# First-layer value weights loaded from GpSimd's queue, and an exponential of one element before the first conversions, in a two-layer attention kernel

## The chip, the cores and the metric

The kernel runs on one core of a Trainium2 chip. The metric is the time of one execution on the device, in microseconds (us). A core has five engines that run side by side: TensorE (PE in the profile; its weight loads are a row of their own, PEld), VectorE (DVE), ScalarE (ACT), GpSimd (POOL) and SyncE (SP). Transfers between the chip's memory and the core's are issued by SP, ACT and POOL, each from a queue of its own, and are carried by 16 DMA engines that all queues share.

## The reference, cut to what matters

Two attention layers over 4 images of 4096 tokens with 256 channels; all numbers are fp32.

```python
# layer 0
q, k, v = x @ Wq + bq, x @ Wk + bk, x @ Wv + bv       # 256 -> 32, 32, 256
attn = softmax(q @ k.T)                               # 4096 x 4096 for each image
x = gamma * (attn @ v) + x
# layer 1
f, g, v = x @ Wf + bf, x @ Wg + bg, x @ Wh + bh       # 256 -> 32, 32, 128
beta = softmax(g @ f.T)
x = x + (beta @ v) @ Wo + bo
```

The weights matter here: Wq and Wk of layer 0 hold 32 KB each, Wv of layer 0 holds 256 KB, Wh of layer 1 holds 128 KB.

## The kernel before, in words

The work of an image and layer is cut into steps: a block of queries (256 in layer 0, 512 in layer 1) against a group of keys. A step computes scores on PE (line 638), exponentials on ACT (a reduced-precision "high" part at line 648 and the whole at 655), differences on DVE (676, 681), and sums weighted by the values on PE (706, 730). From step 8 on the order of all instructions is the order in which the program writes them (`MANUAL_FROM = 8`, line 1138 and around); ahead of that a scheduler orders them, engine by engine, and it also chooses the semaphores that DMAs raise. The queues of SP and ACT share eight such semaphores, and the queue of POOL has eight more; each is used in turn, and an issue whose semaphore still belongs to an earlier DMA waits until that one has landed.

The change lies in the lead, the part before the first scores. There the kernel

- loads the first 8 tiles of tokens from SP (`load_first`, line 311, 128 KB each); tiles 0 and 1 form half-block 0, tiles 2 and 3 half-block 1, and so on;
- makes an identity matrix on POOL (`make_identity`, masks.py:197 and 199);
- loads the weights in the loop of lines 340 to 355: for layer 0 from ACT's queue, for layer 1 from POOL's. In each turn the weights of queries and keys go into one tile `wqk_whole` (line 345), the biases into `bqk` (346), ACT rounds the tile to a "high" part (349), DVE forms the rest (350), and the weights of values are loaded (354). Lines 356 to 358 load three small tensors of layer 1 from POOL;
- for each half-block transposes the tokens on PE (417, result `psx`), copies them to `xT` on ACT (418), rounds them to `xh` on ACT (435), forms `xl` on DVE (438), and projects them: queries and keys on PE (456, `psqk`, from `xh` and `xl` with `wqk`), values on PE (507, `psv`, from `xT` with `wv`);
- takes the projections out: queries and keys by ACT (472), DVE (476), ACT (479) and DVE (483), after which eight small DMAs from POOL spread them into `k` and `q` (line 560); values by ACT (537) and DVE (550, 551).

So ACT's first instructions, before the change, are its issues of Wq, bq, Wk, bk and Wv, then the load of its function table, then the conversion at line 349. In PE's order the first projection of values (507) stands behind the transposes of half-blocks 0 and 1 and ahead of the first projection of queries and keys (456), with which it is interleaved. In ACT's order the value take-out of half-block 0 (537) stands ahead of the second rounding of its queries and keys (479).

The change also names `seen_v`, a small tile that line 333 sets to zero and in which line 517 later notes sizes of values, and `down`, one number per partition that line 332 sets to -2^-13.

Of the kernel before, what the change touches and what calls it, by code (L numbers as in the profile page):

```python
# [50 lines left out]
F32 = mybir.dt.float32  # L51
F32R = mybir.dt.float32r
I32 = mybir.dt.int32
AF = mybir.ActivationFunctionType
# [3 lines left out]
P = 128  # L58
# [192 lines left out]
def fast_path(ctx: ExitStack, tc: tile.TileContext, x, w0, w1, wo, bo, gamma, out, off):  # L251

    nc = tc.nc
    B, N, C = x.shape
    NCC = C // P
    NB = N // QB
    D = w0[0].shape[1]
    CV = (w0[4].shape[1], w1[4].shape[1])
# [14 lines left out]
    const = ctx.enter_context(tc.tile_pool(name="const", bufs=1))  # L273
# [56 lines left out]
    seen_v = const.tile([P, 2, NH], F32, name="seen_v")  # L330
    down = const.tile([P, 1], F32, name="down")
# [4 lines left out]
    wqk, bqk, wv = [], [], []  # L336
    bv1 = const.tile([P, 1], F32, name="bv1")
    gamma_sb = const.tile([P, 1], F32, name="gamma")
    wo_sb = const.tile([P, C], F32, name="wo")
    for l, (q_w, q_b, k_w, k_b, v_w, v_b) in enumerate((w0, w1)):  # L340
        queue = (nc.scalar, nc.gpsimd)[l]
        w_sb = work.tile([P, NCC, 2 * D], F32, tag="small", bufs=4, name=f"wqk_whole{l}")
        b_sb = const.tile([P, 1], F32, name=f"bqk{l}")
        for g, w_dram, b_dram in ((0, q_w, q_b), (D, k_w, k_b)):
            queue.dma_start(w_sb[:, :, g : g + D], w_dram.rearrange("(c p) d -> p c d", p=P))
            queue.dma_start(b_sb[2 * D + g : 3 * D + g, :], b_dram.rearrange("(d o) -> d o", o=1))
        w_parts = const.tile([P, NCC, 4 * D], F32R, name=f"wqk{l}")
        high, low = w_parts[:, :, : 2 * D], w_parts[:, :, 2 * D :]
        nc.scalar.copy(high, w_sb)
        nc.vector.tensor_sub(low, w_sb, high.bitcast(F32))  # L350
        wqk.append(w_parts)
        bqk.append(b_sb)
        v_sb = const.tile([P, NCC, CV[l]], F32, name=f"wv{l}")
        queue.dma_start(v_sb, v_w.rearrange("(c p) d -> p c d", p=P))
        wv.append(v_sb)
    nc.gpsimd.dma_start(bv1, w1[5].rearrange("(c o) -> c o", o=1))
    nc.gpsimd.dma_start(wo_sb, wo)
# [675 lines left out]
    for n, s in enumerate(steps):  # L1033
        now[0] = n
        b, l, j = s.b, s.l, s.j
# [105 lines left out]
def tile_two_attention_layers(tc: tile.TileContext, *args):  # L1141
    nc = tc.nc
    with tc.tile_pool(name="flag", bufs=1) as pool:
        off = pool.tile([1, 1], I32, name="off")
        fast_path(tc, *args, off)
        flag = nc.values_load(off[0:1, 0:1], min_val=0, max_val=4 * P, skip_runtime_bounds_check_because="a count")
        with tc.If(flag < 1, preferred_fallthrough_block=False, label="in_range") as usual:
            pass
        with usual.Else():
            general_path(tc, *args)  # L1150
# [40 lines left out]
```

## Time and profile before

| what | value |
|---|---|
| median of 3 runs | 3091.56 us (3089.11 to 3091.99) |
| the profiled execution's own time | 3090.12 us |
| its span in the trace | 3088.3 us |
| granted TensorE clock, mean | 0.998 |
| PE busy | 3062.8 us, 99% of the span |
| DVE busy | 2765.4 us, 90% |
| ACT busy | 2196.2 us, 71% |
| POOL busy | 772.2 us, 25% |
| ACT_TABLE_LOAD in the whole run | 1, of 1.28 us |

Times in the trace count from the start of the span. The views used are: the page's busy times; the timeline, which gives start, length, engine, line, operation and tiles of each group, and in brackets the engine's idle time before it with what ended it; the table of DMA issues, with each transfer's size and its time from issue to landing; busy time by stretches; and the chain of work that ended last. Rows whose engine ends in q (ACTq, SPq) are issues of transfers. "x4" means that a row merges four instructions.

### The profile page before, as it was taken

The numbers are of one execution on the slowest core, as the hardware profiler recorded it, in microseconds if no ns is written. First come the engines' busy times: TensorE is split into PE (matmuls) and PEld (weight loads), VectorE is DVE, ScalarE is ACT, GpSimd is POOL, SyncE is SP. The second block draws the span as 40 slices with busy tenths as digits, with TensorE's granted clock in tenths as the row PEclk, the third lists the DMA queues.
The fourth block names the chain that finished last, engine by engine and source line by source line (L and its number), as shares of the span: only waits on it lengthen the run. The fifth ranks groups of instructions, "written<-read, shape, count | busy, mean of one in ns | idle before, by whom it ended". The sixth has DMA issues, their size and how long they took to land.

```text
span 3088.3 us, 55083 instructions
## 1 busy us (share of the span) xinstructions
PE 3062.8 (99%) x19866; PEld 2664.2 (86%) x19866; DVE 2765.4 (90%) x3366; ACT 2196.2 (71%) x2900; POOL 772.2 (25%) x1136
## 2 busy tenths in 40 slices
PE   8999999999999999999999999999999999999998
PEld 7999998666799999866689999976668999997665
DVE  7889989999898999999989998999998888889997
ACT  6777777777677777777767677777776666667775
POOL 5111113222421111422241111132234111123332
PEclk9999999999999999999999999999999999999999
DMA  5344445666644444656664444466666333335666
GB/s 134 77 90 88 90 88 117 140 134 137 130 89 90 88 91 87 130 132 137 133 126 92 87 91 88 90 132 130 139 131 118 65 68 73 60 76 118 126 135 142
DMA packets 460902, 331.09 MB, mean 107 GB/s; under 512 B 266610, under 2 KB 404212, under 8 KB 460628
## 3 DMA queue, kind: packets, MB, share of 16 engines
q0 software_dynamic: 109248, 185.47, 33.5%
q1 hardware_dynamic: 350180, 141.47, 18.5%
q8 instruction: 160, 2.62, 0.4%
q14 instruction: 114, 0.93, 0.1%
q10 hardware_dynamic: 1200, 0.59, 0.1%
HBM read 136.58 MB, written 103.61 MB: 78 GB/s over the span
## 4 chain that ended last, share of the span: by engine, by line
PE 90%; DVE 5%; DMA 2%; issue 1%; ACT 1%; POOL 0%; ACTq 0%; DVEq 0%; POOLq 0%
PE acc_pair L706 23%; PE acc L706 23%; PE acc L730 21%; PE st L638 14%; PE psv L507 4%; PE psqk L456 2%; PE pso L838 2%; DMA p_sum_moved<-p 2%; DVE p_sum L695 1%; DVE low L676 1%; DVE d L681 1%; ACT p L655 0%; DVE v0l L681 0%; DVE v0h L676 0%; DVE v0d L676 0%
## 5 line engine op out<-in xcount | busy, mean ns | idle before, releaser
L648 ACT ACTIVATE high<-st,down 128x1024 fp32r<-128x1024 f32 x651 | 727.4, 1117 | 656.4 <-PE st L638 555.2
L655 ACT ACTIVATE p<-st 128x1024 f32<-128x1024 f32 x1024 | 1022.4, 1020 | 30.6 <-DMA p_sum_moved<-p 21.5
L676 DVE TENSOR_TENSOR low<-p,high 128x1024 fp32r<-128x1024 f32 x559 | 683.1, 1222 | 114.6 <-ACT p L655 111.1
L681 DVE SCALAR_TENSOR_TENSOR d<-low,high 128x1024 fp32r<-128x1024 f32 x543 | 662.7, 1220 | 14.6
L638 PE MATMUL st<-q,k 128*128 128x256 f32 (+1 forms) x3072 | 660.3, 323 | 2.2 <-ACT p L655 2.1
L638 PEld LDWEIGHTS st<-q,k 128*128 128x128 f32 x3072 | 469.0, 188 | 60.1 <-issue 13.6
L730 PE MATMUL acc<-p,v 128*128 128x512 f32 (+1 forms) x1028 | 481.4, 590 | 0.2
L706 PE MATMUL acc<-v0d,d 128*128 128x258 f32 x2048 | 336.6, 286 | 0.6 <-DVE d L681 0.6
L706 PE MATMUL acc<-v0h,high 128*128 128x258 f32 x2048 | 329.9, 283 | 0.3 <-ACT o L787 0.3
L706 PE MATMUL acc_pair<-v0h,high 128*128 128x258 f32 x2048 | 330.1, 283 | 0.0
L706 PE MATMUL acc_pair<-v0d,d 128*128 128x258 f32 x2048 | 329.9, 283 | 0.0
L706 PE MATMUL acc_pair<-v0l,low 128*128 128x256 f32 (+1 forms) x2048 | 325.4, 281 | 0.0
L706 PE MATMUL acc<-v0l,low 128*128 128x256 f32 (+1 forms) x2048 | 324.8, 280 | 0.0
L730 PEld LDWEIGHTS acc<-p,v 128*128 128x128 f32 x1028 | 193.2, 189 | 142.6 <-issue 122.8
L771 POOL DMA_DIRECT2D out<-x x128 | 114.4, 894 | 803.2 <-DVE x L765 787.8
L695 DVE TENSOR_TENSOR p_sum<-p_sum,p 128x1024 f32<-128x1024 f32 x253 | 308.4, 1219 | 0.3
L669 POOL DMA_DIRECT2D p_sum_moved<-p x160 | 141.3, 883 | 580.4 <-DMA p_sum_moved<-p 198.4
L706 PEld LDWEIGHTS acc<-v0d,d 128*128 128x128 f32 x2048 | 282.2, 190 | 3.0 <-DVE d L681 1.6
L706 PEld LDWEIGHTS acc<-v0h,high 128*128 128x128 f32 x2048 | 282.3, 190 | 2.1 <-ACT o L787 1.6
L706 PEld LDWEIGHTS acc_pair<-v0h,high 128*128 128x128 f32 x2048 | 281.4, 189 | 0.1
L706 PEld LDWEIGHTS acc_pair<-v0d,d 128*128 128x128 f32 x2048 | 280.7, 189 | 0.1
L706 PEld LDWEIGHTS acc_pair<-v0l,low 128*128 128x128 f32 x2048 | 277.3, 188 | 0.0
(179 smaller groups left out, 4284.1 us busy)
## 6 DMA issues: line engine op xcount, KB each, us to landing
p_sum_moved<-p POOLq DMA_DIRECT2D x193, 512.0 KB, 4.9
x_res<-in_x SPq DMA_DIRECT2D x128, 128.0 KB, 3.2
qk_dram<-qk_parts SPq DMA_DIRECT2D x128, 128.0 KB, 2.0
x_res<-bias POOLq DMA_DIRECT2D x128, 128.0 KB, 4.1
out<-bias SPq DMA_DIRECT2D x128, 128.0 KB, 4.3
out<-x POOLq DMA_DIRECT2D x128, 128.0 KB, 3.1
q<-qk_dram POOLq DMA_DIRECT2D x252, 64.0 KB, 3.8
out<-y POOLq DMA_DIRECT2D x124, 128.0 KB, 4.2
```

The costliest lines, as they stand in the source:

```text
L456: nc.tensor.matmul(t["ps"], wqk[l][:, c, :], x_parts[key][n][:, c, :], start=(c == n == 0), stop=(c == NCC - 1 and n == 1),)
L507: nc.tensor.matmul(ps[:, n, :], xT[key][:, c, n * P : (n + 1) * P], wv[l][:, c, :], start=(c == 0), stop=(c == NCC - 1),)
L638: nc.tensor.matmul(st[:, g, :], k_t[b, l, kt // NT][:, kt % NT * P : (kt % NT + 1) * P], q_t[b, l, j * n // QB][:, q0 : q0 + n], start=Tru ...
L648: nc.scalar.activation(self.high, s_flat, AF.Exp, bias=down)
L655: nc.scalar.activation(self.p, s_flat, AF.Exp)
L669: nc.gpsimd.dma_start(moved_sums[b, j, order % both], self.p, accum_op=ALU.add)
L676: nc.vector.tensor_sub(self.low, self.p, self.high.bitcast(F32))
L681: nc.vector.scalar_tensor_tensor(self.d, self.low.bitcast(F32), -UP, self.high.bitcast(F32), ALU.mult, ALU.add)
L695: nc.vector.tensor_add(p_sum, other, self.p)
L706: nc.tensor.matmul(acc[2 * s + which][:, :width], p[:, g, s * P : (s + 1) * P], v0[self.i][v][:, g, :width], start=self.first and what != ...
L730: nc.tensor.matmul(acc[which].rearrange("p (a n) -> p a n", n=QB0)[:, cols, :], v_part[:, g, :], p[:, g * NS : (g + 1) * NS, :][:, cols, : ...
L771: nc.gpsimd.dma_start(out_rows(b, j, s), x_new, accum_op=ALU.add)
```

## The change

The weights of layer 0's values move ahead of the loop and to POOL's queue. In the loop the two weights of queries and keys are issued first and the two biases after them, for both layers. Between them, for layer 0, ACT computes one exponential per partition from `down` into the first column of `seen_v`, which line 517 overwrites later. Layer 1's weights of values stay where they were.

```diff
+    v0_sb = const.tile([P, NCC, CV[0]], F32, name="wv0")
+    nc.gpsimd.dma_start(v0_sb, w0[4].rearrange("(c p) d -> p c d", p=P))
     for l, (q_w, q_b, k_w, k_b, v_w, v_b) in enumerate((w0, w1)):
         queue = (nc.scalar, nc.gpsimd)[l]
         w_sb = work.tile([P, NCC, 2 * D], F32, tag="small", bufs=4, name=f"wqk_whole{l}")
         b_sb = const.tile([P, 1], F32, name=f"bqk{l}")
-        for g, w_dram, b_dram in ((0, q_w, q_b), (D, k_w, k_b)):
+        for g, w_dram in ((0, q_w), (D, k_w)):
             queue.dma_start(w_sb[:, :, g : g + D], w_dram.rearrange("(c p) d -> p c d", p=P))
+        if l == 0:
+            nc.scalar.activation(seen_v[:, 0, :1], down, AF.Exp)
+        for g, b_dram in ((0, q_b), (D, k_b)):
             queue.dma_start(b_sb[2 * D + g : 3 * D + g, :], b_dram.rearrange("(d o) -> d o", o=1))
...
-        v_sb = const.tile([P, NCC, CV[l]], F32, name=f"wv{l}")
-        queue.dma_start(v_sb, v_w.rearrange("(c p) d -> p c d", p=P))
+        v_sb = v0_sb if l == 0 else const.tile([P, NCC, CV[l]], F32, name=f"wv{l}")
+        if l == 1:
+            queue.dma_start(v_sb, v_w.rearrange("(c p) d -> p c d", p=P))
         wv.append(v_sb)
```

In the scheduled program of the changed kernel ACT's queue begins with Wq, Wk, the table load, the exponential, bq, bk and then the conversion of line 349. POOL's order is: fill of the identity, Wv, the select that finishes the identity, Wg, Wf, bg, bf, Wh, then as before. On PE ten of the first 80 matrix instructions change places, and on DVE and SP a few of the first instructions do (on SP the store of the identity goes ahead of a bias load, and some token tiles ahead of stores); behind that each engine's order is the same in both kernels, and so are the waits, up to the numbering of the semaphores.

## The prediction

> **What bounds the kernel now.** I read the page's busy times first.
>
> ```profile
> PE 3062.8 (99%) x19866; PEld 2664.2 (86%) x19866; DVE 2765.4 (90%) x3366; ACT 2196.2 (71%) x2900; POOL 772.2 (25%) x1136
> ```
>
> PE is idle for 3088.3 - 3062.8 = 25.5 us in all, and the change touches nothing behind the first microseconds: from about the 80th matmul on the scheduled orders are the same. So I ask only how much earlier the lead can hand over to a body that PE fills. Next the timeline of PE (its column: start, length):
>
> ```profile
> 3.32 1.30 PE L417 MATMUL psx<-ident,x_nat 128*128 128x128 f32 x4 [3.32 <-DMA x_nat<-in_x]
> 5.05 1.34 PE L417 MATMUL psx<-ident,x_nat 128*128 128x128 f32 x4 [0.42 <-DMA x_nat<-in_x]
> 8.29 1.19 PE L507 MATMUL psv<-wv,xT 128*128 128x256 f32 x2 [1.90 <-ACT xh L435]
> 8.92 0.78 PE L456 MATMUL psqk<-xh,wqk 128*128 128x256 f32 x1
> 9.49 1.05 PE L507 MATMUL psv<-wv,xT 128*128 128x256 f32 x2
> 9.99 0.78 PE L456 MATMUL psqk<-xl,wqk 128*128 128x256 f32 x1
> 10.56 0.41 PE L456 MATMUL psqk<-xh,wqk 128*128 128x256 f32 x1
> ...
> 13.64 0.28 PE L456 MATMUL psqk<-xl,wqk 128*128 128x256 f32 x1
> ```
>
> PE ends the second transposes at 5.05 + 1.34 = 6.39 and then stands for 1.90 us before the first value projection. The bracket blames the rounding to xh, but psv reads wv and xT, not xh. So I looked at the transfers: issue on ACT, and time to landing.
>
> ```profile
> wv<-in_L_conv_Wv ACTq DMA_DIRECT2D x1, 256.0 KB, 4.8
> wo<-in_L_conv_Wo POOLq DMA_DIRECT2D x1, 128.0 KB, 4.2
> wqk_whole<-in_L_conv_Wg POOLq DMA_DIRECT2D x1, 32.0 KB, 3.4
> wqk_whole<-in_L_conv_Wk ACTq DMA_DIRECT2D x1, 32.0 KB, 3.7
> ```
>
> ```profile
> 0.84 0.46 ACTq L345 DMA_DIRECT2D wqk_whole<-in_L_conv_Wq  x1
> 1.33 0.48 ACTq L346 DMA_DIRECT2D bqk<-in_L_conv_bq  x1
> 1.43 0.88 POOL L345 DMA_DIRECT2D wqk_whole<-in_L_conv_Wg  x1 [0.40 <-issue]
> 1.84 0.45 ACTq L345 DMA_DIRECT2D wqk_whole<-in_L_conv_Wk  x1
> 3.39 0.38 ACTq L354 DMA_DIRECT2D wv<-in_L_conv_Wv  x1
> 3.80 1.28 ACT L349 ACT_TABLE_LOAD   x1 [3.80 <-DMA wqk_whole<-in_L_conv_Wq]
> 5.60 0.30 ACT L349 CAST wqk<-wqk_whole 128x128 fp32r<-128x128 f32 x1 [0.51 <-DMA wqk_whole<-in_L_conv_Wk]
> 5.80 0.58 ACT L418 COPY xT<-psx 128x512 f32<-128x512 f32 x1
> ```
>
> Wv lands at 3.39 + 4.8 = 8.19, and PE starts 0.1 us later. xT was there at 5.80 + 0.58 = 6.38. So the wait is for Wv. It went out late because its issue stood behind four others and, I infer, waited for Wq's landing (0.84 + 2.5 = 3.3), whose semaphore it takes over.
>
> Last, the chain of work that ended last, in order of time, for what hangs on this start:
>
> ```profile
> 11.19 1.72 PE psv L507 x4
> 12.93 0.60 ACT v0h L537
> 13.55 0.41 ACT qk_parts L479
> ```
>
> psv of half-block 0 ends at 12.9; ACT waits for it, and only behind it rounds queries and keys, which start POOL's eight spreading DMAs at 14.24. These go out until 18.15 and take 2.6 us to land (20.75); at 20.87 ACT uses their buffer again. All of that hangs on when psv starts.
>
> **The change part by part.**
>
> *Wv on POOL's queue.* It takes the place of Wg, first on POOL: issue at 1.43 instead of 3.39, 1.96 us earlier. With its own 4.8 us it lands at 6.23. Bounds: not before 4.83, where the 32 KB of Wg landed from this slot; not after 9.9, where Wo, the last large load of this queue, landed (5.69 + 4.2). I take 6.23, since the 4.8 are those of the same bytes. PE then is held by what is next: xT (below, 5.95) and its own transposes (6.39). So psv starts at 6.39 + 0.1 = 6.5: 8.29 - 6.5 = **1.8 us earlier**.
>
> *The cost in the shared DMA engines.* From 4 to 8 us they are 0.97 to 0.99 busy, and now 256 KB come in ahead of token tiles 2 and 3, which held the second transposes for 0.42 us. All of Wv ahead of them would be 256 KB at 294 GB/s (the stretch 6 to 8) = 0.9 us; none, 0. I take 0.3, a third, because the queues of SP and ACT carry bytes beside it. Net **1.5 us**.
>
> Here the Trainium skill speaks against the change: DMA: Bandwidth & Descriptors, "Issuing engines are not separate DMA queues", says that all issuers share the same 16 engines and that spreading issues over several saves the sequencer's time alone. By that the move would be worth 1.96 us of issue at most, and nothing in bandwidth. The busy share of 0.99 agrees.
>
> *Wk ahead of bq.* Wk takes bq's slot: 1.84 to 1.33, 0.5 us earlier, landing at 1.33 + 3.74 (its row in the chain) = 5.07. The conversion goes from 5.60 to about 5.1, xT from 6.38 to 5.1 + 0.30 + 0.58 = 5.95, xh to 6.6, xl (0.69) to 7.3. The second matmul of queries, third on PE from 6.5, needs xl at 7.6, so it is ready. This gain is needed so that xT does not take Wv's place, but adds nothing to the 1.8.
>
> *The exponential.* It pulls the table load from 3.80 to about 1.85, ending at 3.1. The load ended at 5.08 before, 0.5 us ahead of Wk's landing, so it was hidden: worth nothing. Its own length has no row; between 0.15 us (the one-element conversion at line 896) and 0.37 us (an ACTIVATE of 128x256) it is done by 3.5. It fits in a wait of ACT that lasts to 5.07. Without that cover it would cost 1.6 us. There is still one table load, with the same table, so no function needs another.
>
> *The biases, and POOL's other loads.* bq and bk go out at about 3.5 and 4.0 instead of 1.33 and 2.31; at 3.5 us to landing they are there by 7.5, and DVE's line 476 needs them at 11.62 - 1.5 = 10.1. Cover 2.6 us. Wg and Wf now queue behind Wv on POOL; Wf goes from 3.17 to about 3.4 and, at 4.1 us to landing plus up to 0.9 behind Wv, lands between 7.5 and 8.4. ACT's second conversion, at 7.41 before, waits for it, and xh of half-block 1 behind it; but ACT's next (472) waits for PE until about 9.7, and PE reads that xh at 13.40 - 1.5. Hidden. The identity stays where it was, behind one POOL issue. bv, Wo and gamma come about 0.7 us later; DVE reads them behind work that is not due.
>
> *SP.* Token tile 8 was issued at 8.21, just behind Wv's landing at 8.19: it appears to take over Wv's semaphore. It now follows a bias, landed by about 7.5. Tile 6 now follows Wk instead; both feed transposes past 10 us. Nothing is lost.
>
> **Sum.** 1.8 - 0.3 = 1.5 us, carried by the chain above into a body that is PE-bound and unchanged. Against the profiled execution: 3090.12 - 1.5 = **3088.6 us**. That execution is 1.4 under the median of the runs shown and 1.0 over their lowest.
>
> **The rivals.**
>
> *The clock comes up sooner.* The same 256-column matmul takes 0.78 us at 8.92 and 9.99, 0.41 at 10.56 and 0.28 at 13.64, though the granted clock of these stretches reads 1.00. So PE is slow from 8.29 to 10.5, 2.2 us. If it is a pause of PE that makes it slow, a start at 6.5 with hardly a pause halves that: 1.1 more, 2.6 in all, **3087.5**. If the rise falls at the same instant, 10.5, PE does 4.0 us of slow work instead of 2.2: (4.0 - 2.2) / 2 = 0.9 gained, 3089.2. The Trainium skill (TensorE: Matmul & The Clock Gate, Part 1) has a gate that opens after about 3.4 us of sustained activity, in a window that runs freely. By it either end is possible; no run here shows the window.
>
> *POOL's queue is served late.* From 3 to 6 us its packets took 7.6% of the DMA engines, against 51% for SP's. If Wv keeps to such a share, it lands with the last loads, at 9.9, psv starts at 10.0, 1.7 us late: **3091.8, slower**. It decides from a landing after 8.19. Against it: POOL had little but 128-byte pieces out then, and had up to 74% from 7.5 to 8 once Wh and Wo were moving.
>
> *Hidden anyway.* The chain passes through ACT, DVE, POOL's issues and token tiles before PE fills up (PE is idle 0.75 of 4 us from 20, 0.31 from 24). If one of those has its own time, the gain is eaten: **3090.1**. For it: ACT is busy 3.88 of 4 us from 20. Against: all of them start from line 479, which moves along.
>
> **How the numbers follow.** Forecast 0.45, clock sooner 0.15, hidden 0.15, late 0.14, and 0.11 for something no row shows (0.07 faster, 0.04 slower by over 0.2%). 0.2% is 6.2 us, about what a measurement of this kernel can tell from no change; all four named cases lie within it. Range: low end 3090.1 - 2.9 (1.8 + 1.1) less the 1.0 by which runs lie under the profiled one, 3086; high end 3091.8 plus the 1.9 by which the highest run lies over it, 3093.7.
>
> **What would show it.** Right: Wv issued on POOL near 1.4 and landed before 7; psv's first matmul near 6.5 with hardly idle time before it; line 479 near 12.0; the first scores (20.42) near 19; the same PE busy time in the body. Wrong: psv later than 8.3 with Wv landing last; second transposes past 5.9; a wait at line 472 or 476 for a bias; more than one table load; or a body that differs.

## The result and the profile after

The changed kernel takes **3086.85 us** (median of 22 runs, 3084.45 to 3089.01), the kernel before 3090.99 us (22 runs beside them, 3088.08 to 3093.45). The ratio is 0.9987, 95% interval 0.9981 to 0.9992: 4.1 us less, under 0.2%. That is inside the range of the prediction, near its low end of 3086, and 2.7 times the 1.5 us that it forecast. The profiled execution took 3085.12 us, its span is 3083.3 us; before, they were 3090.12 and 3088.3.

Lines of the changed kernel are six higher than before from the transposes on (417 is 423, 456 is 462, 507 is 513, 655 is 661, 667 is 673). First the busy times on the page of the kernel after.

```profile
PE 3061.6 (99%) x19866; PEld 2665.0 (86%) x19866; DVE 2763.9 (90%) x3366; ACT 2198.8 (71%) x2901; POOL 775.3 (25%) x1137
```

PE's idle time fell from 25.5 to 21.7 us. ACT has one instruction more, and so has POOL: 1137 for 1136, since Wv is now its to issue. The second number decides most of what follows.

The lead, in the timeline of PE and in that of ACT with its issues (kernel after; start, length, engine, line, operation, idle time before):

```profile
6.00 1.15 PE L423 MATMUL psx<-ident,x_nat 128*128 128x128 f32 x4 [1.38 <-DMA x_nat<-in_x]
6.94 1.06 PE L513 MATMUL psv<-wv,xT 128*128 128x256 f32 x2
7.44 0.77 PE L462 MATMUL psqk<-xh,wqk 128*128 128x256 f32 x1
...
9.08 0.41 PE L462 MATMUL psqk<-xh,wqk 128*128 128x256 f32 x1
```

```profile
1.32 0.49 ACTq L347 DMA_DIRECT2D wqk_whole<-in_L_conv_Wk  x1
1.84 1.28 ACT L349 ACT_TABLE_LOAD   x1 [1.84 <-issue]
...
3.13 0.20 ACT L349 ACTIVATE seen_v<-down 128x1 f32<-128x1 f32 x1
3.95 0.30 ACT L354 CAST wqk<-wqk_whole 128x128 fp32r<-128x128 f32 x1 [0.61 <-DMA wqk_whole<-in_L_conv_Wk]
4.65 0.59 ACT L424 COPY xT<-psx 128x512 f32<-128x512 f32 x1 [0.40 <-PE psx L423]
...
12.07 0.40 ACT L485 CAST qk_parts<-qk_parts 64x256 fp32r<-64x256 f32 x1
```

And its table of DMA issues (KB, us to landing):

```profile
wv<-in_L_conv_Wv POOLq DMA_DIRECT2D x1, 256.0 KB, 4.3
...
wqk_whole<-in_L_conv_Wk ACTq DMA_DIRECT2D x1, 32.0 KB, 2.5
```

Wv goes out at 1.43 and lands at 5.73. psv now follows the second transposes without idle time, at 6.94 instead of 8.29. What is late next is token tiles 2 and 3: PE stands for 1.38 us before the transposes that need them, which begin at 6.00 instead of 5.05.

To see how far this carries I compared, exponential by exponential (the 1024 of line 655, then 661), how much earlier each begins than in the kernel before. The first begins 1.22 us earlier, the 8th 0.87, the 65th 0.85, the 705th and still the 759th 1.09; in between it wanders (1.95 at the 256th). At the 760th alone it jumps to 3.99, at the 769th it is 4.50, and it stays near that to the end (4.53 at the last). The last stretch but one shows it in busy times too. Rows of kernel before, then after, over the same work (the columns: the stretch, its length, busy us of PE, PEld, DVE, ACT and POOL, clock, DMA share, GB/s):

```profile
84.00:2300.00 2216.00, 2211.22 (x14476) 1934.01 (x14475) 2020.46 (x2424) 1602.06 (x2131) 527.27 (x759) 1.00 0.54 110
2300.00:2350.00 50.00, 47.13 (x178) 31.36 (x177) 40.02 (x42) 33.39 (x47) 28.80 (x49) 1.00 0.71 145
```

```profile
83.10:2298.90 2215.80, 2211.70 (x14476) 1934.38 (x14476) 2019.52 (x2424) 1603.81 (x2131) 528.98 (x759) 1.00 0.54 110
2298.90:2345.50 46.60, 46.17 (x178) 31.73 (x177) 39.93 (x42) 33.64 (x47) 28.86 (x49) 1.00 0.76 155
```

178 matmuls each, in 50.0 us and in 46.6: PE's idle time there was 2.87 us and is 0.43; the other 0.96 of the 3.4 us lie in rows that the view counts as busy. So most of the gain lies 2300 us behind the change, among instructions that it does not touch. What happens there is on POOL. Kernel before, then after:

```profile
2306.95 4.61 POOL L560 DMA_DIRECT2D k<-qk_dram  x8
2316.00 0.56 POOL L667 DMA_DIRECT2D p_sum_moved<-p  x1 [4.45 <-issue]
2316.55 1.96 POOL L560 DMA_DIRECT2D k<-qk_dram  x4
2321.23 0.92 POOL L669 DMA_DIRECT2D p_sum_moved<-p  x1 [2.72 <-DMA p_sum_moved<-p]
...
2327.95 0.92 POOL L669 DMA_DIRECT2D p_sum_moved<-p  x1 [3.82 <-DMA p_sum_moved<-p]
```

```profile
2305.89 4.12 POOL L566 DMA_DIRECT2D k<-qk_dram  x7
2310.68 0.50 POOL L566 DMA_DIRECT2D k<-qk_dram  x1 [0.68 <-DVE v0l L687]
2313.45 0.56 POOL L673 DMA_DIRECT2D p_sum_moved<-p  x1 [2.27 <-ACT p L661]
...
2317.15 0.92 POOL L675 DMA_DIRECT2D p_sum_moved<-p  x1 [1.19 <-ACT p L661]
...
2323.08 0.92 POOL L675 DMA_DIRECT2D p_sum_moved<-p  x1 [3.01 <-DMA p_sum_moved<-p]
```

Eight k loads go out evenly before; after, the eighth is late (the bracket names `v0l` of DVE, which this load does not read). In exchange the first `p_sum_moved`, which copies an exponential away, is not. The pair of exponentials ahead of it on ACT, and the copy in the table of DMA issues, before and after:

```profile
2312.64 1.93 ACT L655 ACTIVATE p<-st 128x1024 f32<-128x1024 f32 x2
p_sum_moved<-p POOLq DMA_DIRECT2D x1, 512.0 KB, 4.6
```

```profile
2311.55 1.93 ACT L661 ACTIVATE p<-st 128x1024 f32<-128x1024 f32 x2
p_sum_moved<-p POOLq DMA_DIRECT2D x1, 512.0 KB, 3.1
```

Before, the second of the pair ended at 2314.57 (2312.64 + 1.93), and the copy went out 1.43 us later, for the blame "issue", that is for nothing the profile names. After, it ends at 2313.48 (2311.55 + 1.93) and the copy goes out with its end. The copy also lands sooner, 3.10 us from its issue for 4.62. Together this is 1.43 + 1.52 = 2.95 us, and the 760th exponential, the next one that waits for this copy, gains 2.90. Why the late copy takes longer to land is open. The next ones add into the same place (lines 667 and 669), so each waits for the one before to land, and ACT waits with the next exponential until the copy of an earlier one has landed. ACT and PE, kernel before, in that order:

```profile
2320.73 1.03 ACT L655 ACTIVATE p<-st 128x1024 f32<-128x1024 f32 x1 [2.79 <-DMA p_sum_moved<-p]
...
2327.45 1.02 ACT L655 ACTIVATE p<-st 128x1024 f32<-128x1024 f32 x1 [2.71 <-DMA p_sum_moved<-p]
```

```profile
2328.52 0.72 PE L638 MATMUL st<-q,k 128*128 128x512 f32 x2 [1.20 <-ACT p L655]
```

After, ACT waits 0.23 us at the second place, and this wait of PE is gone. Over the whole body the views of waits (us, times, longest), first before, then after, have:

```profile
ACT p L655 <- DMA p_sum_moved<-p: 21.5, 12, 3.0
...
PE st L638 <- ACT p L655: 2.1, 2, 1.2
```

```profile
ACT p L661 <- DMA p_sum_moved<-p: 12.2, 10, 2.8
```

**Why one issue is late.** When POOL's DMAs are numbered in the trace, one is late at regular places. At numbers 371, 613, 734 and 1097 of the kernel before a spreading load of k or q (line 560) stands directly behind another, and goes out 1.60, 1.55, 1.52 and 1.72 us behind it; the places are 121 apart or multiples of it. Elsewhere this kernel has 451 such pairs, and in 420 the distance is under 0.8 us. Late pairs elsewhere move with the program: those at 171, 443, 715 and 987 (1.84 us each) are at 172, 444, 716 and 988 in the kernel after (1.76 to 1.83). In the twelve traces of this study (before, after and ten experiments) 55 such pairs fall on the series 129 + 121 n, and all 55 are 1.43 us apart or more (the most 3.31). It is not the wait for one semaphore: POOL's eight are used in turn, and 121 is 15 times eight and one, so each late place uses another.

Number 855 is also in the series. Before, 855 is the `p_sum_moved` of 2316.00; with one more DMA ahead, it is the k load of 2310.68. The twelve traces agree: in the four kernels where 855 is this copy it goes out 1.43 or 1.44 us behind the end of the exponential and takes 4.4 to 5.0 us to land; in the eight others it goes out within 0.03 us of that end and takes 2.9 to 3.1. Not every place of the series costs time: number 250 of the kernel after, a copy at 647.23, goes out as the wait ahead of it ends.

### The profile page after: what moved, and what is told of

The parts are those of the page before. It is cut to its first block, busy times and chain, and to the rows that moved or that the text cites. A ratio compares the mean times of both kernels' runs of the same rounds, so it can differ in the third digit from the quotient of the medians.

```text
span 3083.3 us, 55085 instructions
## 1 busy us (share of the span) xinstructions
PE 3061.6 (99%) x19866; PEld 2665.0 (86%) x19866; DVE 2763.9 (90%) x3366; ACT 2198.8 (71%) x2901; POOL 775.3 (25%) x1137
## 4 chain that ended last, share of the span: by engine, by line
PE 90%; DVE 5%; DMA 2%; issue 1%; ACT 1%; POOL 0%; SPq 0%; DVEq 0%; POOLq 0%; ACTq 0%
PE acc_pair L712 23%; PE acc L712 23%; PE acc L736 22%; PE st L644 14%; PE psv L513 5%; PE psqk L462 2%; PE pso L844 2%; DMA p_sum_moved<-p 1%; DVE p_sum L701 1%; DVE d L687 1%; DVE low L682 0%; ACT p L661 0%; DMA x_nat<-in_x 0%; DVE v0h L682 0%; DVE v0l L687 0%
```

## The experiments

Two theories stood against each other. *Count*: the change puts one DMA more ahead of everything on POOL, so the late places fall one DMA earlier, and the stall near 2316 goes. *Start*: the earlier lead, by whatever it moves relative to memory traffic, avoids it. The table gives all kernels: by how much the 8th, 705th and 769th exponential begin earlier than in the kernel before (one trace each), the step between the last two, and the difference of the timed medians beside each other with the ratio's 95% interval. A kernel whose interval holds 1 is not told apart from the kernel before by its time. The two traces of the kernel before differ by 0.73 us at the 8th exponential, so smaller differences between leads are not told from chance.

| kernel | 8th | 705th | 769th | step | us timed | interval |
|---|---|---|---|---|---|---|
| the change | 0.87 | 1.09 | 4.50 | 3.41 | -4.1 | 0.9981 to 0.9992 |
| after_again | 0.99 | 1.25 | 5.09 | 3.84 | -2.7 | 0.9980 to 0.9999 |
| before_again | -0.73 | -1.18 | -1.09 | 0.09 | 0.0 | 0.9993 to 1.0012 |
| before_one_more | 0.20 | -0.62 | 3.44 | 4.06 | -3.5 | 0.9979 to 0.9997 |
| after_one_less | -3.28 | -5.11 | -3.71 | 1.40 | -1.4 | 0.9984 to 1.0002 |
| after_zero_bg | 2.20 | 1.05 | 1.11 | 0.06 | -1.7 | 0.9987 to 1.0005 |
| after_six_more | -6.88 | -6.80 | -1.72 | 5.08 | +1.3 | 0.9993 to 1.0011 |
| after_twelve_more | -11.59 | -11.82 | -8.31 | 3.51 | +8.9 | 1.0016 to 1.0039 |
| wv_alone | -1.31 | -3.10 | 0.85 | 3.95 | -2.0 | 0.9984 to 1.0003 |
| after_no_exp | 1.34 | -0.06 | 3.63 | 3.69 | -4.6 | 0.9975 to 0.9993 |
| after_late_biases | 1.11 | 1.06 | 5.73 | 4.67 | -4.5 | 0.9976 to 0.9994 |

**One more DMA, and nothing else of the change** (before_one_more):

```diff
+    for n in range(1):
+        nc.gpsimd.dma_start(const.tile([P, 1], F32, name=f"spare{n}"), gamma.partition_broadcast(P))
```

> The kernel before, with one more transfer of 0.5 KB on POOL's queue in the lead (gamma loaded a second time into a tile that nothing reads). Theory 'count': in both traces POOL's 129th transfer and every 121st behind it go out 1.1 to 1.5 us late, and before, one of these slots falls on the first p_sum_moved of a block at 2316.00, which costs about 3.3 us of PE time; one more transfer in the lead shifts the slots by one transfer, so that it falls on a k load. Then this kernel gains about 3.3 us (2 to 4.5) over before although its lead is the same (gain at the first exponential within 0.3 us of zero). Theory 'start': the gain is that of the lead alone, so this kernel is as before, within 1 us.

The lead is the old one (0.20 us), and the step is there, 4.06 us. POOL in this kernel:

```profile
2307.59 4.11 POOL L562 DMA_DIRECT2D k<-qk_dram  x7
2312.61 0.50 POOL L562 DMA_DIRECT2D k<-qk_dram  x1 [0.90 <-DVE v0l L683]
2315.17 0.56 POOL L669 DMA_DIRECT2D p_sum_moved<-p  x1 [2.07 <-ACT p L657]
```

This is the picture of the changed kernel, from 0.5 KB that nobody reads. *Start* can't give it. Its time, 3.5 us under the kernel before, is not told apart from that of the change.

**One DMA less than the change** was tried in two ways. In after_one_less gamma is loaded from ACT's queue:

```diff
-    nc.gpsimd.dma_start(gamma_sb, gamma.partition_broadcast(P))
+    nc.scalar.dma_start(gamma_sb, gamma.partition_broadcast(P))
```

> The changed kernel with gamma loaded from ACT's queue instead of POOL's, so that POOL issues as many transfers as before the change. Theory 'count': the slots fall where they fell before, the first p_sum_moved near 2315 goes out late again, and only the lead's gain is left: about 0.9 us over before (0.3 to 1.5). Theory 'start': the lead is that of the changed kernel, so the gain is that of the changed kernel, about 4.1 us.

The experiment disturbed what it should have kept: ACT stood on the issue of gamma (6.55) ahead of the first `xT` (6.95 instead of 4.65), and the lead was lost. The step is 1.40 us, neither theory's number, though the first `p_sum_moved` of the block was late again, by 1.44 us. The offsets show where the 1.40 lies: none at the 760th exponential (0.38 lost), 1.01 at the 762nd, where the next `p_sum_moved` landed after 5.12 us (6.1 to 6.5 in the three other kernels with the late copy), and 0.84 at the 769th, whose cause is open. So this kernel does not tell the theories apart by its time. In after_zero_bg one bias of layer 1 is set to zero by DVE instead of loaded, so this kernel leaves the load of bg out:

```diff
+            if l == 1 and g == 0:
+                nc.vector.memset(b_sb[2 * D + g : 3 * D + g, :], 0.0)
+                continue
```

> The changed kernel with one transfer less on POOL and nothing added to another queue: the load of bg, layer 1's first bias, is left out and its 32 numbers are set to zero by DVE (they are zero in the inputs). POOL then issues as many transfers as before the change. Theory 'count': the slots stand where they stood before the change, so the late one falls on the first p_sum_moved near 2315 again; the lead is that of the changed kernel; about 0.9 us (0 to 2) under before. Theory 'start': 4.1 us under before, as the changed kernel.

```profile
2305.91 4.62 POOL L569 DMA_DIRECT2D k<-qk_dram  x8
2314.95 0.56 POOL L676 DMA_DIRECT2D p_sum_moved<-p  x1 [4.42 <-issue]
```

Here the lead is the best of all (2.20 us), and yet the late place is back on the `p_sum_moved` and the step is 0.06. Its time, 1.7 us under the kernel before, is within the 0 to 2 of *count*. Together with before_one_more the two factors are apart: old lead with the count gives the step, new lead without it does not.

**More spare loads** (six and twelve, written as the one above, behind the load of gamma of the changed kernel):

> The changed kernel with six more transfers of 0.5 KB on POOL's queue in the lead (gamma loaded six more times into tiles that nothing reads), in the time in which POOL waits for the first k anyway. Theory 'count': the late slots move to loads of q and k and to stores (near 270, 629, 891, 1303, 1575, 2022, 2307, 2707 and 2973), none to a p_sum_moved; so the stall near 2320 stays away and two slots on p_sum_moved near 648 and 1324 go too: as the changed kernel or up to 1.5 us faster, 4 to 5.6 us under before. Theory 'start': the lead is not better, six issues of 0.5 us more on POOL; the changed kernel's time or a little longer, up to 1 us.

> The same with twelve more transfers. POOL's issues in the lead then take 12 x 0.5 = 6 us more and end near 13.5 instead of 7.5, a little past the first k at 12.77. Theory 'count': two late slots fall on accumulations again, near 1293 and 2301, so this is slower than the one with six more, by 1 to 4 us, and at least 0.5 us of it shows as a lost lead between 1290 and 1310 or between 2300 and 2330 in the trace. Theory 'start': slower than the changed kernel by the 0.5 to 1 us of the lead alone, with no step in the body.

The steps came, 5.08 and 3.51 us, as the late place is off the block's first `p_sum_moved` in both. Two expectations failed. The lead was not free: 6.9 and 11.6 us were lost, because POOL's eight semaphores go round and the spreading loads of the lead then wait for spare loads to land. And where I expected a new loss, a late place on some other `p_sum_moved`, none showed; only the first of that block was seen to cost. In all, the kernel with six more is 1.3 us above the kernel before, where *count* had 4 to 5.6 us under it, and the one with twelve more is 8.9 above.

**The kernel before and the changed one again** (before_again, after_again, unaltered):

> The kernel before, unchanged, for a second profile. Theory 'count': the first p_sum_moved near 2316 goes out late again and PE stands near 2328 again, as in the first profile; the wait near 559 that the first profile has (1.2 us) and the other profiles have less of may or may not come back. Theory 'start': stalls of the body come and go by chance, so the one near 2320 has no reason to come back. Its time is that of before within 1 us.

> The changed kernel once more, unaltered, for a second profile of it. Count theory: the first p_sum_moved of the block near 2313 us goes out without the late slot again and the step there is again +3.4 us within 0.7; the lead is 0.9 us within 0.5. Start theory: the step does not recur, and the offset at the end is the lead's, 0.9 us.

Before, the late `p_sum_moved` recurs (2317.18, after 4.44 us idle) and the step is 0.09; after, it is 3.84. So it belongs to the program and not to one execution. The offsets in between do wander by chance: the two traces of the kernel before differ by 1.3 us between the 385th and the 449th exponential, more than the lead gain. That the lead's 0.87 us reaches the end is therefore not shown by the times.

**The parts of the change.** wv_alone has Wv on POOL's queue alone, with weights and biases in the old order and no exponential; after_no_exp drops only the exponential:

```diff
-        if l == 0:
-            nc.scalar.activation(seen_v[:, 0, :1], down, AF.Exp)
```

> Only the move of Wv to POOL's queue; the exponential and the new order of weights and biases are left out. Theory 'count': one more transfer on POOL, so the body's gain of about 3.3 us is there whatever the lead does; 3 to 4.5 us in all. Theory 'start': the lead's gain depends on Wk's earlier landing and the table load as well, so less than the change's 4.1 us, by up to the 0.5 us of Wk's slot and more.

> The changed kernel without the exponential of one element, so that the table load stands ahead of the first conversion again, behind the biases' issues. By the prediction the load is hidden (ends near 4.1) until Wk lands; in the trace of the changed kernel the conversion started at 3.95, so it may now start up to 0.4 us later, but xT is held by the transposes until 4.65. Both theories: the same time as the changed kernel, within 1 us, and the first exponential of the body within 0.3 us.

Moving Wv alone loses 1.31 us in the lead. Its step came, 3.95 us, but its time is 2.0 us under the kernel before and not the 3 to 4.5 expected, and its interval holds 1. ACT of wv_alone, then of after_no_exp:

```profile
6.92 1.28 ACT L351 ACT_TABLE_LOAD   x1 [6.92 <-DMA wqk_whole<-in_L_conv_Wk]
8.21 0.30 ACT L351 CAST wqk<-wqk_whole 128x128 fp32r<-128x128 f32 x1
```

```profile
3.93 1.28 ACT L352 ACT_TABLE_LOAD   x1 [3.93 <-DMA wqk_whole<-in_L_conv_Wk]
5.22 0.30 ACT L352 CAST wqk<-wqk_whole 128x128 fp32r<-128x128 f32 x1
```

With Wk issued at 1.83, behind Wv's 256 KB (1.43), it took 5.0 us to land; in the change it goes ahead, at 1.32, and takes 2.5. The kernel without the exponential differs from wv_alone in the order of weights and biases alone, and its 8th exponential begins 2.65 us earlier (1.34 for -1.31). So the order of the loads is what makes the move of Wv worth something in the lead. And in both kernels the table load now waits for Wk instead of Wq, so that its 1.28 us come on top of the landing. Without the exponential that costs 1.27 us at the conversion (5.22 for 3.95) and 0.49 at psv (7.43 for 6.94); 0.36 of this are the second transposes, which wait for their token tiles and begin at 6.36 for 6.00. The late tiles cover the rest. It is no longer seen at the 8th exponential (1.34 without it, 0.87 with it), nor in the time: 4.6 us under the kernel before without it, 4.1 with it, with intervals that overlap. At the first exponential 0.3 us was expected at most; it is 0.44, within the 0.73 by which two traces of one kernel differ.

The Trainium skill (ScalarE: Activation LUTs, What ACT_TABLE_LOAD costs) gives about 1283 ns for the load, which agrees with the 1.28 us here, and about 1380 ns of draining beside it for each switch of tables. On this first load no run here shows the second part: the conversion begins 0.01 us behind the load's end.

**A version that might beat both** (after_late_biases). Two small loads of layer 1 go behind gamma on POOL's queue, with the same count:

```diff
-        for g, b_dram in ((0, q_b), (D, k_b)):
-            queue.dma_start(b_sb[2 * D + g : 3 * D + g, :], b_dram.rearrange("(d o) -> d o", o=1))
+        def load_biases(b_sb=b_sb, queue=queue, both=((0, q_b), (D, k_b))):
+            for g, b_dram in both:
+                queue.dma_start(b_sb[2 * D + g : 3 * D + g, :], b_dram.rearrange("(d o) -> d o", o=1))
+
+        if l == 0:
+            load_biases()
...
+    put(9, "a", load_biases)
```

> The changed kernel with the second layer's two 0.5 KB bias loads put behind gamma on POOL's queue instead of near the head of it; POOL issues as many DMAs as in the changed kernel. Count theory: the late slot stays on the k load ahead of the block's first p_sum_moved, so the step near 2310 us stays at +3.4 to +4 us. Shared-lead part: with fewer small loads ahead of the x tiles the lead should lie between the 0.87 us of the changed kernel and the 2.2 us of the kernel without one of the loads, and then 4.3 to 6.2 us below the kernel before, 0 to 2 us below the changed kernel. Start theory: only the lead would carry through, 0.9 to 2.2 us below the kernel before.

3085.55 us (3083.58 to 3087.30), against 3087.31 for the changed kernel and 3090.04 for the kernel before on the same chip. It has the lowest median, but its interval overlaps that of the changed kernel, and its lead (1.11 us) is not clearly better: it beats the kernel before, and is not told apart from the change. Its step, 4.67 us, is above the 3.4 to 4 expected. Why the lead of after_zero_bg was 2.20 is open.

## Why the prediction was right, and where it was wrong

The time came out 1.8 us under the 3088.6 of the prediction, and more than half of the change was for a reason that it did not have. That it lies inside the range is luck: the low end took in the 1.1 us of the rival on the clock, which were not gained, and the spread of the runs. Two of the prediction's own signs of being wrong appeared, second transposes past 5.9 and a body that differs. By its steps:

- *Wv on POOL's queue, 1.8 us*: Wv landed at 5.73 where 6.23 was taken, so the step held with room. The rival that POOL's queue is served late is out.
- *The cost in the shared DMA engines, 0.3 us*: mis-sized. Of the bounds 0 and 0.9 it took a third; the second transposes began 0.95 us later (6.00 for 5.05), the full upper bound. psv started at 6.94, not 6.5. So Wv's early bytes held up those of the tiles. The Trainium skill (DMA: Bandwidth & Descriptors, "Issuing engines are not separate DMA queues") says that transfers of all issuers interleave on the same 16 engines. The 0.95 us agree with it.
- *Net 1.5 us*: psv came 1.35 earlier, line 479 (now 485) at 12.07, near the 12.0 foreseen, the first scores at 18.85 for 20.42. From these 1.57 us it shrank to 0.87 at the 8th exponential. The chain of the kernel after goes there through the landing of a token tile (11.88 to 14.71) and of spreading loads of k (17.68 to 19.60, 23.92 to 26.97), no longer through the value take-out of line 537. So the rival *hidden anyway* was right in part.
- *Wk ahead of bq, nothing of its own*: the gain was larger than the 0.5 us of its slot. It landed at 3.8 where 5.07 was taken, and wv_alone beside after_no_exp shows that without it the move is a loss in the lead.
- *The exponential, worth nothing*: no gain could be measured, but the reason given, a load hidden ahead of Wk's landing, was that of the old order. In the new one Wk lands at 3.8 and the load, left alone, follows it, ending at 5.21; the late tiles are what covers it.
- *The clock comes up sooner*: the slow matmuls lasted from 6.94 to 9.08, 2.1 us for 2.2 before. The rise moved with the work, from 10.56 to 9.08, so neither of the two cases (1.1 us more, or 0.9 in all) happened; that 0.9 is near the 0.87 measured is chance.
- *"carried by the chain above into a body that is PE-bound and unchanged"*: this is the step that failed. The order was unchanged, the body was not: one issue more on POOL moved every late place by one, and one of them had been stalling ACT and PE near 2316. It is worth 3.4 us in the first trace of the change, 3.8 in its second and 4.1 with the spare load alone. The prediction had counted POOL's instructions in the page (1136) without asking what one more does to those behind.

Adding up, 0.87 + 3.41 = 4.3 us, against 4.1 timed. This sum leaves out how the offsets wander between the 8th and the 705th exponential, by up to 1.8 us (after_one_less). For seven of the other ten kernels the offset at the 8th exponential plus the step also lies within 0.9 us of the timed change. The three others miss by 1.3 to 3.3 us: after_again and after_late_biases, whose profiled execution was their fastest, and after_one_less, whose profiled execution was its slowest.

## What to carry to other kernels

An edit in the lead can pay or cost far behind it, without any change of order, by shifting the count on a queue: compare the traces work by work, not only the stretch that was edited. Before a load is moved to an earlier slot, ask whose bytes it takes on the shared engines, and send the small one that is needed first ahead of it. A difference of a few microseconds in thousands can be of a place that one spare DMA moves, so an edit should be tried with the count put back before its own reason is believed.

## What the runs showed of the hardware

POOL's DMA issues have a late place at regular distance. In all twelve traces it fell on numbers 129 + 121 n, wherever two spreading loads stood back to back there (from 129 to 1097): 1.43 to 3.31 us from one issue to the next, 53 of 55 at most 2.18, instead of about 0.5. It follows the number of DMAs: with six or twelve more ahead, the places stayed at the same numbers and fell on other transfers. What POOL does there no view shows: its row is idle, and the cause of the pause is open. That one DMA can delay the next was also seen in the lead: with twelve spare loads six of the first eight spreading loads waited for a spare load to land, and they went out up to 1.8 us apart.
